# Adding the experts' rows straight into the output tensor, with the seldom steps' branch moved into the last sure step

## The chip, the core and the metric

The kernel runs on one core of a Trainium2 chip. Its engines work side by side, each through its own list of instructions in order: PE (TensorE, matmuls; its weight loads are a row of their own, PEld), DVE (VectorE), ACT (ScalarE), POOL (GpSimd) and SP (SyncE, which here only issues transfers). Engines wait for each other through semaphores. The metric is the time of one execution on the device in microseconds (us); the median of three runs stands for the kernel before.

## The reference: what is computed

One decoder layer on `x` of 8 batch rows x 256 tokens x 256 features, and a context of the same shape, all float32:

```python
x = x + linear_attention(layernorm(x))                   # 16 heads, phi(q), phi(k) = elu + 1
x = x + cross(layernorm(x), ctx)                         # l2norm(q) * sum(l2norm(k) * v) @ Wfc + ctx
residual = x
xn = layernorm(x) * gamma + beta
probs = softmax(xn @ Wg.T)                               # 8 experts
top1, top2 = the two likeliest experts; gates g1, g2 = their shares of p1 + p2
out = x + layernorm(x) + sum over e of gate[e] * (gelu(xn @ W1[e] + b1[e]) @ W2[e] + b2[e])
```

Each token goes to exactly two of eight experts, so the last part is 4,096 pairs of a token and an expert, each a product with a 256 x 1024 and a 1024 x 256 matrix. Only the last sum, `residual + out`, is touched by the change: how the experts' rows reach the output.

## The kernel before

**Rows, then steps.** The first part goes through the batch rows (256 tokens each) in a software pipeline: a loop over rounds `i` from 1 to 7 (L1011) calls the stages of rows `i`, `i-1`, `i-2` and `i-3` one after another. PE, DVE, ACT and SP keep the order of the source; POOL's order is chosen by the compiler, save where `in_turn` (L289) ties an instruction to the one before it. The second part is a list of steps (`steps`, L930): in each, 128 pairs of one expert are pushed through both matrices. Steps are interleaved into the last rows' stages by `meanwhile`, and then run alone.

**Slots.** `rank` (L690) counts on PE how many earlier tokens chose each expert, and `place` (L703) turns that into a slot number: 2,048 slots for each of 8 experts, 128 to a tile. Four indirect transfers from POOL per batch row (`slots<-pay,posi`, L726) write token number and gate into the slots. Slots that nobody fills keep what `empty_slots` (L239) wrote at the start: token numbers 2048 to 2175, which are 128 rows of padding behind the real ones, and gate 0.

**A step** s: `fetch_slots` (L844) loads 128 slots, `fetch_weights` (L852) loads the expert's first matrix (1 MB) and second bias; `gather` (L865) collects the 128 token rows from `rows_d`, a DRAM copy of the normalised rows; `turn` (L872) transposes them on PE; eight `first_chunk` (L887) matmul pairs with a gelu on ACT each; eight `second_chunk` (L905) matmuls, run one step later, chunk by chunk between the next step's first chunks; `add_out` (L914) adds the bias on DVE, scales by the gate on ACT, and an indirect transfer from POOL adds the 128 rows into `acc` (L921). `acc` is a DRAM buffer of 2,048 + 128 rows that `base` (L598) has filled with x + layernorm(x) before. An add must wait until the add before it has landed, since both may hold the same token.

**The end.** There can be 32 to 39 steps, as the tokens fall. The first 36 are always run (`SURE`, L927; a step too many works on empty slots). After them every engine reads the number of steps (L1137) and jumps over the three seldom steps if it is 36 or less (L1141), as with this input. Then SP copies `acc` into the output, 2 MB from DRAM to DRAM (L1150), and the program closes (recorded under L1182): SP waits for all transfers, all engines drain and meet.

The functions that the change touches, and what calls them:

Of the kernel before, what the change touches and what calls it, by code (L numbers as in the profile page):

```python
# [29 lines left out]
def decoder_kernel(  # L30
# [59 lines left out]
    rows_d = dram.tile([NTOK + P, D], F32, name="rows_d")  # L90
    acc = dram.tile([NTOK + P, D], F32, name="acc")
# [97 lines left out]
    zero = const("zero", [P, D])  # L189
# [6 lines left out]
    def iota_f(t, shape, pattern):  # L196
        ti = const(t.name + "_i", shape, I32)
        nc.gpsimd.iota(ti, pattern=pattern, base=0, channel_multiplier=0)
        nc.vector.tensor_copy(t, ti)
# [38 lines left out]

    def empty_slots():  # L239

        nc.gpsimd.memset(pads, 0)
        nc.gpsimd.iota(pads[:, :, 0], pattern=[[1, P]], base=NTOK, channel_multiplier=0)
        nc.gpsimd.memset(zero, 0.0)
        nc.sync.dma_start(slots[0 : NTILE - 1, :], pads[:, :, :].rearrange("p r c -> p (r c)"))
        nc.sync.dma_start(
            slots[NTILE - 1 : NTILE, :], pads[0:1, :, :].rearrange("p r c -> p (r c)")
        )
        nc.sync.dma_start(rows_d[NTOK:, :], zero)
        nc.sync.dma_start(acc[NTOK:, :], zero)
# [348 lines left out]
    def base(st):  # L598
        b = st["b"]
        x3 = st["x2"]  # L600
        for t in range(T):
            nc.scalar.activation(
                x3[:, t, :], x3[:, t, :], AF.Identity,
                bias=st["sb"][:, 1, t : t + 1], scale=st["sb"][:, 0, t : t + 1],
            )
        nc.sync.dma_start(tokens(acc, b), x3)
# [6 lines left out]
    puts = []  # L613
# [88 lines left out]

    def place(st):  # L703

        new = named(st)
        at = st["b"] * T
        hot = st["hot"]
        slot = new("slot", [P, T, E])
        nc.vector.tensor_tensor(
            slot,  # L710
            st["prank"].rearrange("p (t e) -> p t e", e=E),
            slot0[:, None, :].to_broadcast([P, T, E]),
            ALU.add,
        )
        nc.vector.tensor_tensor(
            hot, hot, slot[:, :, None, :].to_broadcast([P, T, 2, E]), ALU.mult
        )
        pos = new("pos", [P, T, 2])
        nc.vector.tensor_reduce(pos, hot, axis=AX.X, op=ALU.add)
        posi = new("posi", [P, T, 2], I32)  # L720
        nc.vector.tensor_copy(posi, pos)
        earlier = list(behind)
        behind.clear()
        for t in range(T):
            for c in range(2):
                put = nc.gpsimd.indirect_dma_start(  # L726
                    out=slot_rows,
                    out_offset=bass.IndirectOffsetOnAxis(ap=posi[:, t, c : c + 1], axis=0),
                    in_=pay[:, at + t, c, :], in_offset=None,
                )  # L730
                tc.declare_no_dep(
                    put.ins, group="slots", reason="every token and choice has a slot of its own"
                )
                tc.add_to_no_dep_group("slots", put.ins)
                for name in earlier:
                    tc.add_manual_dep(put.ins, name, ORDERED, reason="in the order of the source")
                puts.append(put.ins.name)
                behind.append(put.ins.name)
# [112 lines left out]

    def fetch_weights(s):  # L852
        e_sp = said(s, 0, ET.SP)
        w1s[s] = mpool.tile([P, KD, F], F32, tag="w1", name=f"w1_{s}", bufs=3)
        nc.sync.dma_start(
            w1s[s], w1_rows[bass.ds(e_sp * D, D), :].rearrange("(k p) f -> p k f", p=P)
        )
        b2s[s] = mpool.tile([P, D], F32, tag="b2", name=f"b2_{s}", bufs=3)
        nc.sync.dma_start(b2s[s], b2_flat[bass.ds(e_sp * D, D)].partition_broadcast(P))

    def reach(s):

        return RA * S if s < NA else NTOK + P
# [8 lines left out]
    def turn(s):  # L872
        p = ps(f"pt_{s}")
        xg = xgs.pop(s)
        for k in range(KD):
            nc.tensor.transpose(p[:, k * P : (k + 1) * P], xg[:, k * P : (k + 1) * P], ident)  # L876
        ready[s] = mpool.tile([P, KD, P], F32, tag="xgT", name=f"xgT{s}")
        for k in range(KD):
            nc.vector.tensor_scalar(  # L879
                ready[s][:, k, :], p[:, k * P : (k + 1) * P],  # L880
                gamma_c[:, k : k + 1], beta_c[:, k : k + 1], op0=ALU.mult, op1=ALU.add,
            )
# [3 lines left out]

    def first_chunk(s, c):  # L887
        if c == CHUNKS[0]:
            hT = mpool.tile([P, FC, P], F32, tag="hT", name=f"hT{s}")
            p = [wide(f"ph_{s}_{i}").rearrange("p (c n) -> p c n", n=P) for i in range(2)]  # L890
            hidden[s] = hT, p, said(s, 0, ET.Activation)
# [3 lines left out]
        for k in range(KD):  # L895
# [5 lines left out]
            hT[:, c, :], p, AF.Gelu_apprx_tanh,  # L901
# [3 lines left out]
    def second_chunk(s, c):  # L905
        if c == CHUNKS[0]:
            summed[s] = ps(f"py_{s}"), said(s, 0, ET.PE)
        p, e_pe = summed[s]
        nc.tensor.matmul(  # L909
            p[:, 0:D], hidden[s][0][:, c, :], w2_flat[:, bass.ds((e_pe * FC + c) * D, D)],  # L910
            start=(c == CHUNKS[0]), stop=(c == CHUNKS[-1]),
        )

    def add_out(s):  # L914
# [6 lines left out]
        in_turn(nc.gpsimd.indirect_dma_start(  # L921
            out=acc[0 : reach(s), :],
            out_offset=bass.IndirectOffsetOnAxis(ap=ids.pop(s)[:, 0:1], axis=0),
            in_=yg[:, :], in_offset=None, compute_op=ALU.add,
        ))
# [4 lines left out]
    def steps(first, last):  # L930
# [3 lines left out]
        for s in range(first, last + 1):  # L934
# [7 lines left out]
            for j, c in enumerate(CHUNKS):  # L942
                took = 0.0
# [14 lines left out]
            yield took  # L958

# [51 lines left out]
    for i in range(1, B):  # L1011
# [7 lines left out]
        run(add_context, i - 2)  # L1019
        run(gates, i - 3)  # L1020
# [9 lines left out]
        run(attend, i - 1)  # L1030
        run(place, i - 3)
        if i > 1:
            run(first_norm, i + 1)
# [14 lines left out]
        if i == 2:  # L1048
            gate_row()
        run(cross_out, i - 2)  # L1050
# [5 lines left out]
        run(key_powers, i)  # L1056
        run(last_norms, i - 2)
        run(attention_out, i - 1)
# [4 lines left out]
        run(turn_last, i - 2)  # L1063
        run(second_norm, i - 1)
# [26 lines left out]
    run(place, p - 1)  # L1091
    run(attended, q)
# [23 lines left out]
    run(place, p)  # L1116
    run(add_context, q, True)
# [15 lines left out]
    run(place, q)  # L1133
    step_end()
    plans["b"] = plan_steps("b", B - 1, NSTEP - NA, other_tiles)
    meanwhile(1e6)
    n_steps = nc.values_load(  # L1137
        total[0:1, 0:1], min_val=0, max_val=NSTEP,
        skip_runtime_bounds_check_because=CLAMPED,
    )  # L1140
    with tc.If(n_steps > SURE):  # L1141
        for s in range(SURE, NSTEP):
            fetch_slots(s)
            fetch_weights(s)
        for s in range(SURE, NSTEP):
            gather(s)
        turn(SURE)
        for _ in steps(SURE, NSTEP):
            pass
    nc.sync.dma_start(out.rearrange("b s d -> (b s) d"), acc[0:NTOK, :])  # L1150

# [34 lines left out]
```

## Time and profile before

| what | value |
|---|---|
| median of 3 runs | 463.07 us (461.97 to 465.4) |
| the profiled execution, its own time | 466.37 us |
| its span in the profile | 464.2 us |
| mean granted TensorE clock | 0.985 |
| PE busy in the span | 435.6 us |
| rounds 3, 4 and 5 over the batch rows | 20.7, 20.8 and 20.7 us |
| a step, from 240 us on | 7.25 us |
| last matmul ends | 447.8 us |
| last add into `acc` starts | 450.30 us |
| copy to the output issued | 454.16 us |

The profile is of one execution, told from the start of its span; the execution's own time is 2.2 us longer, since some of it lies outside the span. PE's matmuls overlap their weight loads, and the ends of matmuls are modelled. [...] A q behind an engine (PEq, POOLq) means its sequencer, which reads instructions ahead of the engine and takes jumps, register loads and drains itself. "Records" are the instructions that the profiler wrote down.

### The profile page before, as it was taken

The page shows a single profiled execution, that of the slowest core. Times are in us where ns is not written, and L with a number is a line of the kernel's source. Part 1 is how long each engine was busy: PE and PEld are TensorE (multiplying, and loading weights), DVE is VectorE, ACT ScalarE, POOL GpSimd, SP SyncE. Part 2 cuts the span into 40 slices and gives each one's busy share as a digit, 9 for nine tenths or more (in the row PEclk, how much of TensorE's full clock was granted, in tenths as well). Part 3 has the DMA queues.
Part 4 walks back from the last instruction along what each step waited for, and adds up shares of the span by engine and source line. Part 5 has one row for each costly group of instructions (what it writes and reads, how often), then busy time and mean ns, then how long its engine had stood idle before and what let it go on. Part 6 is the DMA issues. An engine that isn't in the chain of part 4 may idle for free.

```text
span 464.2 us, 8501 instructions
## 1 busy us (share of the span) xinstructions
PE 435.6 (94%) x2671; PEld 369.7 (80%) x2671; DVE 184.0 (40%) x692; ACT 214.0 (46%) x551; POOL 187.2 (40%) x201
## 2 busy tenths in 40 slices
PE   8889999999999999988999999999999999999950
PEld 5557687776857689877999999899999999999950
DVE  2556778787888767454111110111101111011100
ACT  3526455464636454443444444444444444444420
POOL 6305264536445653635433324333342433333220
PEclk9999999999999999999999999999999999999995
DMA  8604266755604163786677676676757767668225
GB/s 231 202 2 136 69 204 57 217 100 173 137 1 145 28 171 123 182 237 127 157 230 205 177 235 179 200 201 187 233 161 222 194 192 220 185 209 220 41 26 191
DMA packets 48368, 74.36 MB, mean 160 GB/s; under 512 B 9774, under 2 KB 37811, under 8 KB 48291
## 3 DMA queue, kind: packets, MB, share of 16 engines
q1 hardware_dynamic: 39298, 63.10, 46.2%
q0 software_dynamic: 8208, 9.91, 11.3%
q10 hardware_dynamic: 816, 0.79, 0.5%
q8 instruction: 24, 0.39, 0.4%
q14 instruction: 22, 0.17, 0.1%
HBM read 64.44 MB, written 11.44 MB: 163 GB/s over the span
## 4 chain that ended last, share of the span: by engine, by line
PE 86%; DVE 5%; ACT 2%; issue 1%; DMA 1%; POOL 1%; another core or an unknown queue 1%; POOLq 0%; ACTq 0%; DVEq 0%
PE ph L896 28%; PE py L909 26%; PE pxkv L344 6%; PE pkv L344 4%; PE pq L407 3%; PE pq L344 3%; PE po L344 3%; PE pfc L344 3%; PE pt L876 2%; PE pt L338 1%; PE pstate L472 1%; PE pstate L457 1%; DVE qT L421 1%; PE plog L344 1%; PE ptc L338 1%
## 5 line engine op out<-in xcount | busy, mean ns | idle before, releaser
L896 PEld LDWEIGHTS ph<-xgT,w 128*128 128x128 f32 x1152 | 167.2, 191 | 20.2 <-ACT hT L900 4.2
L896 PE MATMUL ph<-xgT,w 128*128 128x128 f32 x1152 | 175.6, 276 | 3.4 <-ACT hT L900 2.4
L909 PE MATMUL py<-w_s,hT 128*128 x576 | 170.7, 380 | 0.0
L900 ACT ACTIVATE hT<-ph,vcols 128x128 f32<-128x128 f32 x288 | 103.0, 367 | 120.5 <-PE ph L896 106.5
L921 POOL DMA_INDIRECT acc<-yg,ids x36 | 57.1, 1586 | 151.3 <-ACT hT L900 113.7
L879 DVE TENSOR_SCALAR xgT<-pt,vcols 128x128 f32<-128x128 f32 x72 | 26.2, 406 | 158.7 <-PE pt L876 150.7
L909 PEld LDWEIGHTS py<-w_s,hT 128*128 128x128 f32 x576 | 88.1, 192 | 0.4
L867 POOL DMA_INDIRECT xg<-rows_d,ids x36 | 36.1, 1002 | 11.7 <-issue 6.2
L726 POOL DMA_INDIRECT slots<-pay,posi x32 | 32.1, 1003 | 10.4 <-issue 7.7
L918 DVE TENSOR_TENSOR y<-py,b 128x256 f32<-128x256 f32 x36 | 15.3, 425 | 44.8 <-ACT hT L900 32.9
L344 PE MATMUL pxkv<-xwkv_s,cT 128*128 128x512 f32 x64 | 31.8, 624 | 0.7 <-ACT cT L378 0.7
L344 PE MATMUL pkv<-wkv_s,hT 128*128 128x512 f32 x64 | 29.9, 593 | 0.0
L920 ACT ACTIVATE yg<-y,ids 128x256 f32<-128x256 f32 x36 | 18.3, 508 | 23.2 <-DVE y L918 21.5
L344 PEld LDWEIGHTS pxkv<-xwkv_s,cT 128*128 128x128 f32 x64 | 12.0, 198 | 10.1 <-issue 8.7
L306 POOL TENSOR_TENSOR rs_b<-ve_b,mhalf 128x2 f32<-128x2 f32 x8 | 8.2, 1021 | 24.4 <-DVE ve_b L319 24.4
L344 PEld LDWEIGHTS po<-wo_s,turnedoT 128*128 128x128 f32 x64 | 12.0, 190 | 7.1 <-ACT turnedoT L508 3.0
L344 PEld LDWEIGHTS pkv<-wkv_s,hT 128*128 128x128 f32 x64 | 11.1, 190 | 8.2 <-issue 8.1
L344 PE MATMUL po<-wo_s,turnedoT 128*128 128x256 f32 x64 | 15.3, 381 | 2.1 <-ACT turnedoT L508 2.1
L407 PE MATMUL pq<-hT,wq_s 128*128 128x256 f32 x64 | 15.2, 381 | 0.6 <-ACT hT L383 0.6
L306 POOL TENSOR_TENSOR rs_a<-ve_a,mhalf 128x2 f32<-128x2 f32 x8 | 5.7, 707 | 24.2 <-DVE ve_a L319 24.2
L344 PE MATMUL pq<-xwq_s,turnedx2T 128*128 128x256 f32 x64 | 15.2, 380 | 0.0
L344 PE MATMUL pfc<-xwfc_s,turnedq2T 128*128 128x256 f32 x64 | 15.2, 380 | 0.0
(193 smaller groups left out, 510.5 us busy)
## 6 DMA issues: line engine op xcount, KB each, us to landing
w<-in_L_ffn_W_dram SPq DMA_DIRECT2D x36, 1024.0 KB
w_s<-in_L_ffn_W_dram SPq DMA_DIRECT2D x8, 1024.0 KB
b<-in_L_ffn_b_dram SPq DMA_DIRECT2D x36, 128.0 KB
x<-in_x_dram SPq DMA_DIRECT2D x8, 256.0 KB
rows_d<-h SPq DMA_DIRECT2D x8, 256.0 KB
acc<-x SPq DMA_DIRECT2D x8, 256.0 KB
c<-in_ctx_dram SPq DMA_DIRECT2D x7, 256.0 KB
ids<-slots SPq DMA_DIRECT2D x36, 1.0 KB
```

Source lines behind the costliest of these rows:

```text
L306: in_turn(nc.gpsimd.tensor_tensor(dst, src, mhalf[:, 0:n], ALU.pow))
L344: nc.tensor.matmul(p[:, 0:width], srcT[:, k, t * P : (t + 1) * P], w[:, k, 0:width], start=(k == 0), stop=(k == KD - 1),)
L407: nc.tensor.matmul(p[:, m, :], wq_s[:, k, m * P : (m + 1) * P], st["hT"][:, k, :], start=(k == 0), stop=(k == KD - 1),)
L726: put = nc.gpsimd.indirect_dma_start(out=slot_rows, out_offset=bass.IndirectOffsetOnAxis(ap=posi[:, t, c : c + 1], axis=0), in_=pay[:, at ...
L867: in_turn(nc.gpsimd.indirect_dma_start(out=xgs[s][:, :], out_offset=None, in_=rows_d[0 : reach(s), :], in_offset=bass.IndirectOffsetOnAxis ...
L879: nc.vector.tensor_scalar(ready[s][:, k, :], p[:, k * P : (k + 1) * P], gamma_c[:, k : k + 1], beta_c[:, k : k + 1], op0=ALU.mult, op1=ALU ...
L896: nc.tensor.matmul(p, w1s[s][:, k, c * P : (c + 1) * P], ready[s][:, k, :], start=(k == 0), stop=(k == KD - 1),)
L900: nc.scalar.activation(hT[:, c, :], p, AF.Gelu_apprx_tanh, bias=vcols[:, bass.ds(e_act * FC + c, 1)],)
L909: nc.tensor.matmul(p[:, 0:D], hidden[s][0][:, c, :], w2_flat[:, bass.ds((e_pe * FC + c) * D, D)], start=(c == CHUNKS[0]), stop=(c == CHUNK ...
L918: nc.vector.tensor_tensor(y, p[:, 0:D], b2s.pop(s), ALU.add)
L920: nc.scalar.activation(yg, y, AF.Copy, scale=ids[s][:, 1:2].bitcast(F32))
L921: in_turn(nc.gpsimd.indirect_dma_start(out=acc[0 : reach(s), :], out_offset=bass.IndirectOffsetOnAxis(ap=ids.pop(s)[:, 0:1], axis=0), in_= ...
```

## The change

Four things change together.

1. `acc` goes. `base` writes x + layernorm(x) into the output tensor itself, the indirect transfers add into it, and the copy at the end is left out. `rows_d` loses its 128 rows of padding too.
2. Since there is no padding row left, an empty slot must name a real token that has nothing to do with the expert's tile, with gate 0: two slots of one transfer must not name the same token. The empty slots of all tiles get tokens 0 to 127 at the start. An expert's first tile can hold some of these for real, so once row 0's choices are known, its 128 slots are filled with tokens of row 0 that did not choose the expert: `without`, `spread` and `fill_spare` find them with DVE comparisons and 16 small bf16 matmuls in round 3, and a transfer writes them. Row 0's puts come after that, in round 4, in two pairs (`put` is split off from `place`).
3. The read of the number of steps and the jump over the seldom steps move from the end into step 35, the last sure one, ahead of its third chunk. The seldom steps run there one after another, with shared buffers (`own`).
4. The program ends with a memset on POOL that waits for the landing of the last add.

```diff
-    rows_d = dram.tile([NTOK + P, D], F32, name="rows_d")
-    acc = dram.tile([NTOK + P, D], F32, name="acc")
+    rows_d = dram.tile([NTOK, D], F32, name="rows_d")
+    out_rows = out.rearrange("b s d -> (b s) d")
...
+        nc.vector.tensor_copy(tok, pay[:, 0:T, 0, 0])
+        iota_f(back, [P, P], [[-1, P]], P - 1)
+        for t in range(T):
+            nc.vector.tensor_tensor(
+                tok_e[:, t],
+                eye8[:, :, None].to_broadcast([P, E, E]),
+                eye8[:, None, :].to_broadcast([P, E, E]),
+                ALU.is_equal,
+            )
+            nc.vector.tensor_scalar_mul(tok_e[:, t], tok_e[:, t], tok[:, t : t + 1])
...
-        nc.gpsimd.iota(pads[:, :, 0], pattern=[[1, P]], base=NTOK, channel_multiplier=0)
-        nc.gpsimd.memset(zero, 0.0)
+        nc.gpsimd.memset(spare, 0)
+        nc.gpsimd.iota(pads[:, :, 0], pattern=[[1, P]], base=0, channel_multiplier=0)
...
-        nc.sync.dma_start(rows_d[NTOK:, :], zero)
-        nc.sync.dma_start(acc[NTOK:, :], zero)
...
-        nc.sync.dma_start(tokens(acc, b), x3)
+        bases.append(nc.sync.dma_start(tokens(out_rows, b), x3).ins.name)
...
+    def without(st):
+        free = small.tile([P, T, E], BF16, tag="free", name="free")
+        nc.vector.tensor_tensor(
+            free,
+            tok[:, :, None].to_broadcast([P, T, E]),
+            st["prank"].rearrange("p (t e) -> p t e", e=E),
+            ALU.subtract,
+        )
+        nc.vector.scalar_tensor_tensor(
+            free, st["both"], -2.0 * S, free, op0=ALU.mult, op1=ALU.add
+        )
+        st["at"] = mpool.tile([P, T, E, P], BF16, tag="w1", name="at", bufs=3)
+        st["free"] = free
+
+    def spread(st, t):
+        nc.vector.tensor_tensor(
+            st["at"][:, t],
+            back[:, None, :].to_broadcast([P, E, P]),
+            st["free"][:, t, :, None].to_broadcast([P, E, P]),
+            ALU.is_equal,
+        )
+
+    def fill_spare(st):
+        p = ps("pspare")
+        for t in range(T):
+            for e in range(E):
+                nc.tensor.matmul(
+                    p[0:E, 0:P], tok_e[:, t, e, :], st["at"][:, t, e, :],
+                    start=(t == 0 and e == 0), stop=(t == T - 1 and e == E - 1),
+                )
+        nc.vector.tensor_copy(spare[:, :, 0], p[0:E, 0:P])
+        nc.sync.dma_start(
+            slots[0 : NTILE - 1, :].rearrange("(e q) c -> e q c", e=E)[:, 0, :],
+            spare.rearrange("e r c -> e (r c)"),
+        )
...
+    def put(st, *ts):
+        at, posi = st["b"] * T, st["posi"]
...
-        in_turn(nc.gpsimd.indirect_dma_start(
-            out=acc[0 : reach(s), :],
+        add = nc.gpsimd.indirect_dma_start(
+            out=out_rows[0 : reach(s), :],
...
+        in_turn(add)
+        sums.append(add.ins.name)
...
             for j, c in enumerate(CHUNKS):
+                if s == SURE - 1 and j == 2:
+                    seldom()
...
+    def seldom():
+        n_steps = nc.values_load(
+            total[0:1, 0:1], min_val=0, max_val=NSTEP,
+            skip_runtime_bounds_check_because=CLAMPED,
+        )
+        with tc.If(n_steps > SURE):
+            for s in range(SURE, NSTEP):
+                fetch_slots(s)
+            for s in range(SURE, NSTEP):
+                gather(s)
+            for s in range(SURE, NSTEP):
+                fetch_weights(s)
+                turn(s)
+                for c in CHUNKS:
+                    first_chunk(s, c)
+                for c in CHUNKS:
+                    second_chunk(s, c)
+                add_out(s)
...
         run(add_context, i - 2)
+        if i == 4:
+            put(rows[0], 0)
...
         run(attend, i - 1)
+        if i == 3:
+            without(rows[0])
         run(place, i - 3)
+        if i > 3:
+            run(put, i - 3)
...
+        if i == 3:
+            spread(rows[0], 0)
         run(cross_out, i - 2)
...
         run(key_powers, i)
+        if i == 3:
+            spread(rows[0], 1)
         run(last_norms, i - 2)
+        if i == 4:
+            put(rows[0], 1)
...
         run(turn_last, i - 2)
+        if i == 3:
+            fill_spare(rows[0])
...
-    n_steps = nc.values_load(
...
-        for _ in steps(SURE, NSTEP):
-            pass
-    nc.sync.dma_start(out.rearrange("b s d -> (b s) d"), acc[0:NTOK, :])
+    nc_last = nc.gpsimd.memset(mhalf, 0.0)
+    tc.add_manual_dep(nc_last.ins, sums[-1], WRITTEN, reason="the last rows are added")
```

## The prediction

> **What bounds the kernel now.** I read the busy times and their slices first, then the last pieces of the chain of waits, then the waits of SP's queue, and last the instructions of the lines that the change moves.
>
> ```profile
> PE 435.6 (94%) x2671; PEld 369.7 (80%) x2671; DVE 184.0 (40%) x692; ACT 214.0 (46%) x551; POOL 187.2 (40%) x201
> ...
> 57.40:78.10 20.70, 20.45 (x108) 15.40 (x108) 16.28 (x65) 11.37 (x29) 11.21 (x13) 1.00 0.59 140
> 119.60:141.70 22.10, 21.23 (x109) 15.33 (x109) 18.88 (x83) 11.30 (x29) 11.27 (x14) 1.00 0.21 46
> 240.00:440.00 200.00, 199.92 (x1377) 184.61 (x1376) 31.60 (x83) 93.05 (x249) 68.92 (x53) 1.00 0.67 192
> ```
>
> The three window rows read: length, then PE, weight loads, DVE, ACT and POOL busy. PE is full in the rounds over the batch rows (20.45 of 20.70) and in the steps (199.92 of 200), so work added to PE costs its own time, and DVE work costs what PE then waits for it.
>
> ```profile
> 445.70 3.86 DMA acc<-yg,ids
> ...
> 450.60 1.25 POOL acc L921
> ```
> ```profile
> SPq L1150 <- DMA acc<-yg,ids: 19.5, 1, 19.5
> ...
> SPq L1182 <- DMA out_dram<-acc: 7.5, 1, 7.5
> ```
>
> After the last matmul (447.8) nothing computes. The add of step 34 lands 3.86 us after its start, at 449.56; the last add starts at 450.30 and lands at 454.16, when SP's wait of 19.5 ends; the copy's issue is 0.61, its landing another 7.5, and the rest to 464.2 is 1.5. From last landing to end: **10.06 us**.
>
> **What goes: the copy (L1150).** All of it lies on the path. What is late next is POOL's own closing:
>
> ```profile
> L1182 POOLq DRAIN  x3: 46/103/5953, 452.7 to 463.9; - x3
> ...
> L1141 POOLq INC_SWDGE_SEM  x1: 1593/1593/1593, 451.1 to 451.1; - x1
> ```
>
> One of three drains takes 5.95 us. It must be the first (at 452.7): a later one would overrun the span. It ends at 458.67, hidden under the copy, and the closing exchange after the copy's landing needs 1.1 from POOL. The change queues it behind a memset that waits for the last landing. Bounds: 0 (it falls away, or runs beside the landing) to 5.95 (it starts after the memset). The nearest row is its own, and it stands behind the memset in POOL's order, so I take 5.95. From last landing to end: 0.4 until the memset has run (0.10 by L141's row, the start as after the add's landing at 449.56, rounded down), 5.95, 1.1, in all 7.45. **Gain 10.06 - 7.45 = 2.6**; with no drain 10.06 - 1.6 = 8.5.
>
> [...]
>
> **What comes: the branch inside step 35.** Before, the jump over the seldom steps came when PE had nothing left to issue:
>
> ```profile
> L1141 PEldq COMPARE_BRANCH  x1: 3634/3634/3634, 444.8 to 444.8; - x1
> L1141 SPq COMPARE_BRANCH  x1: 45/45/45, 431.4 to 431.4; - x1
> ...
> L1141 ACTq COMPARE_BRANCH  x1: 45/45/45, 448.7 to 448.7; - x1
> ...
> q8 instruction: 24, 0.39, 0.4%
> ```
>
> PE's took 3.63 us, the others' 0.05 to 0.07. Queue q8 moved 24 packets of 16 KB, one per some 240 of PE's records (5,779 in all), so it is PE's instruction fetch; a 3.63 us jump is one that waits for such a fetch. The arm skipped is three steps of 110 records and some waits, about 340 records or 1.4 fetches.
>
> At the new place PE's sequencer stands ahead of PE: in the trace the address step of a step's second L909 chunk comes 1.45 us before the weight load that uses it, steady over steps 4 to 34. With that chunk's 0.43 it has 1.88 us in hand. It spends 0.57 until the branch is read (444.24 to 444.81 in the end now), the branch, and 0.3 on the arm's semaphores; the first of these also waits until PE's own matmuls are done. Dear jump: 0.57 + 3.63 + 0.3 - 1.88 = 2.6 of idle PE. Cheap jump: only the emptied pipeline, about 0.17 for the last matmul's end, 0.3 for the semaphores, 0.1 to the next weight load: 0.6. Both rows are near (PE's own; the four others' same instruction). What decides is whether the landing place has been fetched. By record counts the jump now starts about 86 records earlier in its fetched stretch (some 120 records of steps 35 and 36 then come behind it, 34 new ones of the spare rows ahead). [...] I take the cheap one, **0.6**, and keep 2.6 as the upper end, 0.5 as the lower.
>
> [...]
>
> The join's POOL part (TENSOR_LOAD 0.51, INC_SWDGE_SEM 1.59) falls between the adds of steps 33 (438.68 to 440.23) and 34 (445.70): 5.5 us of idle cover it; without it the last two adds come later one for one. ACT's and DVE's 0.4 to 0.9 lie in ACT's 0.51 per chunk and DVE's 6.6 idle.
>
> **What comes: the spare rows, before step 0.**
> - Tables (two copies, four 128x64 operations): DVE 1.2, by six rows of about 0.2 (L219, L228). They stand ahead of k at L446, which waits 0.46 for ACT anyway and must be done by 21.73 for PE's pstate: k ends 21.9 instead of 21.2. **0.25**.
> - Sixteen bf16 matmuls of 128 columns on PE in round 3. No row shows one; fp32 transposes of 128 columns follow each other by 0.11 (four in 0.44), and bf16's weight load is half fp32's (0.096 against 0.19): 0.055 to 0.11 each, 0.9 to 1.8. The load's row is the nearer: **1.1**, all on PE.
> - DVE in round 3: two small operations 0.35, two of 1,024 elements (0.42 at 256 and 0.69 at 512 elements give 1.23 each), a copy 0.2: 3.0 us. The round at 119.6 has the plan's 4.0 us of DVE in one piece and is 1.4 longer than its neighbours. Here it is in four pieces, before PE has taken 1.1 more itself and DVE idles 0.93, 0.53, 1.04 and 0.51: 0 to 1.0, **0.25**.
>
> ```profile
> 76.10 1.07 POOL L306 TENSOR_TENSOR rs_b<-ve_b,mhalf 128x2 f32<-128x2 f32 x1 [3.00 <-DVE ve_b L319]
> ...
> 83.92 0.71 POOL L306 TENSOR_TENSOR rs_a<-ve_a,mhalf 128x2 f32<-128x2 f32 x1 [3.39 <-DVE ve_a L319]
> ```
>
> - Row 0's four puts (1.0 each, 0.3 between) move a round later, two into POOL's 3.39 idle before rs_a, two into the 3.00 before rs_b: 2.6 each, hidden. The first waits for the spare slots' transfer: SP issues it near 78 (the copy's end), between the base rows (75.2) and the next load, whose second half waits until 80.6 now. If it lands by 81, POOL is in time; rs_a, and with it DVE's off and ACT's h, stand behind it. Cost 0; if the cover is gone, up to 2 us.
> - POOL's new iota replaces a memset (0.3) in an idle of 3.96; two 128 KB writes go, at 14.8 and 15.6, with SP idle. 0.
>
> **Sum.** -2.6 + 0.6 + 0.25 + 1.1 + 0.25 = **-0.4 us**: span 463.8 for 464.2, and 466.0 for the profiled execution's 466.37. On the median of 463.07 (the profiled one is 0.7% above it): **462.7**. Bounds with the long drain: 461.9 to 466.
>
> **Rivals.**
> - B1, the drain runs beside the last landing, from the last add's issue: 450.7 + 5.95 + 1.1 = 457.7, plus 2.2 of costs: span 459.9, time 458.8. For it: the drain now begins at 452.7, before the landing at 454.16. Against: POOL's own work had ended at 451.8.
> - B2, the drain is short: 454.16 + 0.5 + 1.3 = 455.9, plus 2.2: span 458.1, **457.0**. For it: two POOL drains take 0.05 and 0.10. Against: they follow one that had just cleared up.
> - C, slower: the jump in step 35 waits for its fetch again. PE stands 2.6, 2.0 more than taken; with the long drain the span is 465.8 and the time **464.7**, +0.3%. It decides as soon as the jump's stall exceeds 1.0. For it: PE's only row. Against: the shift by 86 records.
> - D, it does not do what it says about order: the output is no tile of the pool, so adds might no longer wait for each other. The last would start at 449.1 rather than 450.3: 1.2 less, 461.5. The wait row of 3.0 before L921 would be gone. 1 in 10, within the cases below.
> - E, POOL late in round 4 and the stall handed on through rs_a in each round after: over 5 us, 468.
>
> **How the numbers follow.** Long drain with a cheap jump 0.38 (462.7, its range 461 to 464.5), with a dear one 0.15 (464.7); B1 0.17 (458.8, with a dear jump 460.8); B2 with a cheap jump 0.17 (457.0), with a dear one 0.06 (459.0); E 0.07. About 1% (4.6 us) is what a measurement of this kernel tells from no change. Faster by over 1%, under 458.4: B2 cheap, a quarter of B1 and a third of B2 dear: 0.24. Slower by over 1%: E, 0.07. The rest 0.69. The range, 456.8 to 465.3, leaves out E and the lower half of B2.
>
> **What would show it.** The copy's row is gone, and the wait of 7.5 at L1182. A POOL drain of about 6 us starts after the last landing (B1: earlier; B2: below 0.2). PE's COMPARE_BRANCH is below 0.1 (C: about 3.6), with an idle stretch of 0.6 (C: 2.6) between two L896 groups near 440. Round 3 is 1.1 to 2.1 longer, the others as they were. rs_a still waits for DVE in round 4, not for the slots. I am wrong above all if the drain's 5.95 us does not come back.

## The result and the profile after

The changed kernel took 461.62 us (median of 22 runs, 459.41 to 464.12) where the kernel before took 463.17 (22 runs, 461.23 to 466.71): ratio 0.9956, 95% interval 0.9937 to 0.9976, some 2.0 us less. The forecast was 462.7, range 456.8 to 465.3. The profiled execution has a span of 461.4 (464.2 before).

The page of the changed kernel: sixteen operations of PE, eleven of DVE and two of POOL are what is added, and PE's instruction fetch is 24 packets as before.

```profile
PE 437.3 (95%) x2687; PEld 372.2 (81%) x2687; DVE 187.8 (41%) x703; ACT 214.0 (46%) x551; POOL 187.6 (41%) x203
...
q8 instruction: 24, 0.39, 0.3%
```

**The tail.** The end of the chain of waits (start, length, what), then the rows of the closing lines (what is written from what, minimum, median and maximum in ns, first and last start), then SP's waits (total, times, longest), all of the changed kernel:

```profile
448.47 0.52 ACT yg L997
448.99 1.56 issue
450.55 3.75 DMA out_dram<-yg,ids
...
454.34 0.37 issue
454.70 0.11 POOLq L1289
```
```profile
L1257 POOL MEMSET mhalf<- x1: 101/101/101, 454.7 to 454.7; 128x4 f32 x1
...
L1289 POOLq DRAIN  x3: 46/109/5802, 454.7 to 461.1; - x3
```
```profile
SPq L1289 <- DMA out_dram<-yg,ids: 21.0, 2, 16.5
```

The copy and its wait of 7.5 are gone. The last add lands at 454.30, the long drain starts at 454.70 and takes 5.80, and the span ends at 461.36: 7.05 us from the last landing to the end (10.06 before). The last row says something that the diff does not: SP's closing waits for the same landing by itself, so by this row GpSimd's memset guards nothing that was open. No run leaves it out.

**The branch.** Rows of the branch's line and the stretch of PE around it (start, busy time, in brackets PE's idle time before and what ended it):

```profile
L1048 PEldq COMPARE_BRANCH  x1: 1292/1292/1292, 437.1 to 437.1; - x1
...
L1048 POOLq INC_SWDGE_SEM  x1: 1545/1545/1545, 439.1 to 439.1; - x1
```
```profile
438.12 0.60 PE L986 MATMUL py<-w_s,hT 128*128 x2
439.01 0.68 PE L973 MATMUL ph<-xgT,w 128*128 128x128 f32 x4 [0.30 <-PEq L1048]
```

PE's jump took 1.29 us, neither 0.05 nor 3.63, and PE stood for a moment only. The exact loss: from step 34's first weight load for the second matmul to the last one of all there are 10.25 us here and 9.72 before, so 0.53.

**The spare rows.** The sixteen matmuls in PE's order, then the windows of rounds 3 and 4 as this execution has them (length, then PE, weight loads, DVE, ACT and POOL busy, PE's clock, DMA share, GB/s):

```profile
77.26 0.60 PE L351 MATMUL pt<-ident,h 128*128 128x128 f32 x4
77.79 1.06 PE L744 MATMUL pspare<-at,tok_e 128*8 128x128 bf16 x16
78.78 1.98 PE L357 MATMUL pxkv<-xwkv_s,cT 128*128 128x512 f32 x4
```
```profile
59.40:81.30 21.90, 21.65 (x125) 16.29 (x125) 18.80 (x70) 11.26 (x29) 7.13 (x9) 1.00 0.42 134
81.30:102.00 20.70, 20.45 (x108) 15.41 (x108) 16.29 (x65) 11.37 (x29) 15.43 (x17) 1.00 0.73 152
...
240.00:440.00 200.00, 199.70 (x1376) 184.43 (x1375) 31.55 (x83) 93.00 (x249) 69.44 (x54) 1.00 0.67 192
```

Round 3 is 1.2 us longer than its 20.70 of before, and PE was busy in all of that (21.65 against 20.45). Round 4 has its 20.70 although POOL carries four puts more. GpSimd is still waiting for VectorE, not for the spare slots:

```profile
85.50 0.98 POOL L780 DMA_INDIRECT slots<-pay,posi  x1 [0.30 <-issue]
87.34 0.72 POOL L319 TENSOR_TENSOR rs_a<-ve_a,mhalf 128x2 f32<-128x2 f32 x1 [0.86 <-DVE ve_a L332]
```

So far each term is where the prediction has it. What does not fit is in between. Against the profile of before, steps 0 and 1 of the changed profile are 3.4 us late (start of step 0's second chunks: 181.13 against 177.76), steps 2 and 3 are 2.8 late, and from step 4 on they are 0.04 early. PE was busy 38.69 us of the 40 from 200 to 240, and 37.69 before. Either the steps absorb what the front costs, which would make the spare rows free, or the two executions differ by something that is in neither kernel. That, and the size of each term, is what the experiments are for.

Theory A: the change is worth the sum of tail, branch and sixteen matmuls; the rest of the two profiles' difference is accident. Theory B: something between 190 and 225 us waits for a fixed time and swallows the front's cost.

### The profile page after: what moved, and what is told of

Read it like the earlier page. It is cut to its first block, busy times and chain, and to the rows that moved or that the text cites. A ratio compares the mean times of both kernels' runs of the same rounds, so it can differ in the third digit from the quotient of the medians.

```text
span 461.4 us, 8548 instructions
## 1 busy us (share of the span) xinstructions
PE 437.3 (95%) x2687; PEld 372.2 (81%) x2687; DVE 187.8 (41%) x703; ACT 214.0 (46%) x551; POOL 187.6 (41%) x203
## 5 line engine op out<-in xcount | busy, mean ns | idle before, releaser
L998 POOL DMA_INDIRECT out_dram<-yg,ids x36 | 57.2, 1588 | 147.7 <-ACT hT L977 106.3
L357 PE MATMUL pxkv<-xwkv_s,cT 128*128 128x512 f32 x64 | 30.4, 600 | 0.8 <-DMA xwkv_s<-in_L_xattn_Wv_dram 0.8
L357 PE MATMUL po<-wo_s,turnedoT 128*128 128x256 f32 x64 | 16.7, 408 | 2.1 <-ACT turnedoT L521 2.1
L420 PE MATMUL pq<-hT,wq_s 128*128 128x256 f32 x64 | 16.6, 406 | 0.6 <-ACT hT L396 0.6
L319 POOL TENSOR_TENSOR rs<-ve,mhalf 128x4 f32<-128x4 f32 x8 | 8.3, 1034 | 18.8 <-DVE ve L593 18.8
L377 ACT ACTIVATE h<-x,off,rs_a 128x256 f32<-128x256 f32 x16 | 8.7, 592 | 14.8 <-DVE off L374 14.8
```

What stands on the lines that cost most here:

```text
L319: in_turn(nc.gpsimd.tensor_tensor(dst, src, mhalf[:, 0:n], ALU.pow))
L357: nc.tensor.matmul(p[:, 0:width], srcT[:, k, t * P : (t + 1) * P], w[:, k, 0:width], start=(k == 0), stop=(k == KD - 1),)
L420: nc.tensor.matmul(p[:, m, :], wq_s[:, k, m * P : (m + 1) * P], st["hT"][:, k, :], start=(k == 0), stop=(k == KD - 1),)
L998: add = nc.gpsimd.indirect_dma_start(out=out_rows[0 : reach(s), :], out_offset=bass.IndirectOffsetOnAxis(ap=ids.pop(s)[:, 0:1], axis=0), i ...
```

## The experiments

All ratios are to the kernel before, run on the same chip in the same stretch; its median there was 468.64 us in the first four runs, 467.09 in the next four, 463.18 in the two with 56 and 84 gathers, 465.96 in the last two.

### 1. Both kernels again

`after_again` is the changed kernel and `before_again` the kernel before, without edits.

> The changed kernel once more, beside the kernel before on the same chip, for a second profile of it. Theory A (three terms make the result: tail -2.96, the jump's stall +0.44, the sixteen matmuls of round 3 +1.18, the rest nothing): ratio to before about 0.997, and again a POOL DRAIN of 5.8 us that starts after the last landing, PE's COMPARE_BRANCH near 1.3 us and step 0's second chunks 1.2 us later than before, measured from the start of round 2. Theory B (the steps give the front's cost back, because something from 190 to 225 us waits for a fixed time): PE stands less between 190 and 225 us than it does before, in this profile too, and the ratio is nearer to 0.994.

> The kernel before once more, for a second profile of it. If the 3.4 us of idle PE between 195 and 217 us that its first profile has and the changed kernel's has not (ScalarE standing 2.52 us for something that the profile doesn't name, among others) belongs to the kernel, it is here again; if it was an accident of that execution, PE is busy there for all but some 1.5 us. PE's COMPARE_BRANCH is again near 3.6 us, POOL's first closing DRAIN near 5.95.

The changed kernel: 467.04, ratio 0.997 (0.9941 to 0.9999). The drain is again 5.80 and behind the landing. From 200 to 240 us, changed kernel again and kernel before again:

```profile
200.00:240.00 40.00, 36.73 (x241) 33.25 (x242) 13.09 (x60) 16.96 (x45) 16.20 (x14) 0.96 0.69 168
```
```profile
200.00:240.00 40.00, 36.05 (x235) 31.97 (x234) 14.12 (x62) 16.52 (x44) 16.17 (x14) 0.96 0.72 163
```

Both stand here, by the same stall: ScalarE waits for something that the profile doesn't name and PE with it. ScalarE and PE of the changed kernel, then ScalarE of the kernel before:

```profile
216.76 0.37 ACT L977 ACTIVATE hT<-ph,vcols 128x128 f32<-128x128 f32 x1 [3.23 <-remote]
...
217.18 0.49 PE L973 MATMUL ph<-xgT,w 128*128 128x128 f32 x2 [2.45 <-issue]
```
```profile
219.39 0.37 ACT L900 ACTIVATE hT<-ph,vcols 128x128 f32<-128x128 f32 x1 [3.24 <-remote]
```

It belongs to both kernels, and the first profile of the changed one was an execution without it. Theory B loses its ground: from the first of the four transposes near 200 us to the first of step 5's there were 24.5 us in the first profile of before and 21.6 in that of the changed kernel, but 26.5 in the new profile of either. (`before_again` took 471.56 in its one run; its drain is again 5.95 and PE's jump 3.57.)

### 2. Without the spare rows

```diff
-                if s == SURE - 1 and j == 2:
+                if s == SURE - 1 and j == 5:
...
-        if i == 4:
-            put(rows[0], 0)
...
-        if i == 3:
-            without(rows[0])
         run(place, i - 3)
-        if i > 3:
-            run(put, i - 3)
+        run(put, i - 3)
...
-        if i == 3:
-            fill_spare(rows[0])
```

(the tables, both calls of `spread` and the second `put` of row 0 go in the same way)

> Leaves out the filling of the spare slots: the tables, the free rows, the sixteen matmuls and the slots' transfer, with the first row's puts back in their old round, so that empty slots of the experts' first tiles name other tokens than they should; the branch stands three chunks later in its step, so that PE meets it at the same place of its instruction stream as in the changed kernel. Theory A: round 3 is 1.18 us shorter on PE, every step starts 1.2 us earlier than in the changed kernel, and the time is 1.2 us less, ratio to before about 0.993 (0.994 to 0.991). Rival (the front's cost is absorbed between 190 and 225 us): the steps from 4 on start when they do in the changed kernel, and the time is the same as that of the changed kernel. POOL's puts of the first row are again between 57 and 78 us, and round 4's POOL work is back at 11.1 us.

465.41, ratio 0.9928 (0.9897 to 0.9959): 2.0 us below the changed kernel on the same chip by the two ratios, with intervals that overlap. Round 3 of this kernel:

```profile
59.40:80.10 20.70, 20.45 (x108) 15.40 (x108) 16.26 (x65) 11.37 (x29) 11.16 (x13) 1.00 0.56 140
```

It is 1.2 shorter than the changed kernel's and equal to the 20.70 of before, and the steps keep the lead: over the same transposes near 200 us to step 5's this profile has 26.5 us, as the others of this chip. The front's cost goes through to the end. Theory A holds for round 3: 1.18 us, all of it PE's sixteen matmuls; DVE's work in that round and the moved puts cost nothing that shows.

The tables do cost something, but not in the profile read so far, where PE's clock was halved just ahead of that place, from 18.61 to 22.02 us (last section). The transposes `ptc` near 20 us and the matmuls `pstate` behind them, in the first profile of before and in `dve_end`, a variant of the changed kernel (section 4) whose clock was whole there; last, DVE's k in `dve_end`:

```profile
21.13 0.60 PE L338 MATMUL ptc<-ident,c 128*128 128x128 f32 x4
21.57 1.09 PE L457 MATMUL pstate<-v,k 128*128 128x136 f32 x8
```
```profile
19.60 0.60 PE L351 MATMUL ptc<-ident,c 128*128 128x128 f32 x4
20.15 1.19 PE L470 MATMUL pstate<-v,k 128*128 128x136 f32 x8
```
```profile
19.41 0.69 DVE L459 SCALAR_TENSOR_TENSOR k<-k,tmpexk 128x512 f32<-128x512 f32 x1
```

With the tables ahead of it, k ends at 20.10, and PE's first weight load for `pstate` starts at 20.15 after 0.18 of idle. From these `ptc` to the `ptc` at the start of round 3 there are 36.39 to 36.41 us in the five profiles with tables and a whole clock there, and 36.17 or 36.18 in the two without tables: **0.21 us**. The spare rows as a whole cost 1.4.

### 3. The tail alone

The kernel before, its copy left out; the base rows are written to the output as well as to `acc`, where the experts' sums stay:

```diff
         nc.sync.dma_start(tokens(acc, b), x3)
+        nc.sync.dma_start(out[b].rearrange("(t p) d -> p t d", p=P), x3)
...
-    nc.sync.dma_start(out.rearrange("b s d -> (b s) d"), acc[0:NTOK, :])
+    nc_last = nc.gpsimd.memset(mhalf, 0.0)
+    tc.add_manual_dep(nc_last.ins, sums[SURE - 1], WRITTEN, reason="the last rows are added")
```

> The kernel before with the last copy left out, so that the output holds the rows of the base alone (each base row is written to the output too) and the experts' sums stay in the scratch buffer; a memset on GpSimd waits for the last add's landing, as in the changed kernel. This is the tail's part of the change alone. Theory A: from the last add's start to the end 10.85 us instead of 13.9, a POOL DRAIN of 5.8 to 5.95 behind the memset, 3.0 us less, ratio to before 0.9935 (0.991 to 0.997). Rival (the long drain was a thing of the copy or of the join right ahead of it): no POOL drain above 0.2 us, 8.5 us less, ratio 0.982.

463.43, ratio 0.994 (0.9912 to 0.9969): 2.8 us less. From the last add's start to the end 10.67 us (13.93 in the first profile of before, 13.75 in the second), and the drain stands behind the memset, as long as ever:

```profile
L1186 POOLq DRAIN  x3: 46/109/5802, 452.5 to 458.9; - x3
```

So the tail is worth 2.8 to 3.3, and the drain is no thing of the copy.

### 4. The last wait on VectorE, and the branch at the end

```diff
-    nc_last = nc.gpsimd.memset(mhalf, 0.0)
+    nc_last = nc.vector.memset(upto_a, 0.0)
```

> The wait for the last add's landing is given to a small memset on VectorE instead of GpSimd; all else as in the changed kernel. Theory A (POOL's closing drain is a fixed piece of work of 5.8 us that needs no landing and only stood behind the memset): the drain starts right behind the last add's issue, near 452.1 in the changed kernel's time, ends near 457.9, and the span ends 0.95 later: 2.5 us less than the changed kernel, ratio to before about 0.990. Rival (the drain itself waits for the landing of what POOL has issued): it starts at 452.1 but ends 5.8 after the landing, no gain against the changed kernel.

465.36, ratio 0.9933 (0.9898 to 0.9969). From the last add's start to the end 9.44 instead of 10.81 us: 1.4 less, not the 2.5 expected, and not nothing. (PE's mean clock was 0.975 in the profiled execution; only its tail is read.)

```profile
L1289 POOLq DRAIN  x3: 46/109/8498, 458.6 to 467.9; - x3
```

The record starts 0.23 ahead of the last add's own start (458.79), so it holds the add too. It ends 8.27 after the add's start. If the drain's own part is 5.80 as elsewhere, it begins 2.5 after that start, where I had put it at 1.55, the length of the add's row.

`dve_end` has the same (its memset waits for the add of step 35 and for that of the last seldom step), and the branch behind the last step again:

```diff
-                if s == SURE - 1 and j == 2:
-                    seldom()
     meanwhile(1e6)
+    seldom()
```

> VectorE's memset has the last wait, as in the run before, and the branch stands behind the last step again, as in the kernel before; the spare rows stay. Theory A (the branch inside step 35 costs PE 0.44 us of its own; at the end GpSimd's half of the join, some 2 us, lies beside what GpSimd does anyway for 2.4 us between the last add's start and the 5.8 us of the drain): PE has no gap of 0.86 us between two weight loads in step 35, its COMPARE_BRANCH is 3.6 us again where nothing waits for it, the last add's start to the end stays at 9.4 us, and the time is 0.4 us below the run with VectorE's memset alone: ratio to before about 0.992. Rival (the join on GpSimd puts the drain off one for one): the last add's start to the end is 11.5 us, ratio about 0.997.

464.21, ratio 0.9944 (0.9907 to 0.998): by time not to be told from the run before it. In the trace the two theories part: from the last add's start to the end 9.56 us, so GpSimd's half of the join costs 0.1 at most, and PE has its 9.71 from step 34's first second-matmul load to the last instead of 10.25. With the join ahead of it the drain's row holds the drain alone. It starts right behind INC_SWDGE_SEM, 2.4 after the add's start at 450.07 and ahead of the add's landing at 453.75, and is as long as ever (5.84), so it waits for no landing:

```profile
L1289 POOLq DRAIN  x3: 46/252/5842, 452.5 to 459.4; - x3
...
L1046 PEldq COMPARE_BRANCH  x1: 3574/3574/3574, 444.6 to 444.6; - x1
...
L1046 POOLq INC_SWDGE_SEM  x1: 1593/1593/1593, 450.9 to 450.9; - x1
```

### 5. What a jump costs PE

```diff
-                if s == SURE - 1 and j == 2:
+                if s == SURE - 1 and j == 0:
```

> The branch stands two chunks earlier in step 35, ahead of its first chunk; all else as in the changed kernel. In the six profiles so far PE's jump ended 2.5 to 2.7 us after the first packet of PE's instruction queue for the stretch it lands in, or 0.4 after it began where that packet was long past. In the two profiles of the changed kernel that packet came 1.2 us ahead of the jump, so a jump 1.8 us earlier comes before it. Theory A: PE's COMPARE_BRANCH takes 2.5 to 3.6 us, the sequencer's lead at that place (1.0 to 1.4 us) doesn't cover it, and PE stands 2.2 to 3.3 us in step 35 instead of 0.44. Rival (a jump ahead of the last steps is never dear, whatever has been fetched): 0.4 to 1.6 us and PE stands at most 1.0.

466.81 in one run. Two chunks earlier in the same step the jump is dear, and PE stands for it:

```profile
L1048 PEldq COMPARE_BRANCH  x1: 2892/2892/2892, 437.3 to 437.3; - x1
```
```profile
440.66 0.68 PE L973 MATMUL ph<-xgT,w 128*128 128x128 f32 x4 [2.08 <-PEq L1048]
```

Some 2.3 us lost between the two weight loads (2.65 apart, 0.32 at the same place one step earlier) for 0.53 in the changed kernel. Beside the records of PE's instruction queue q8 the lengths fall in line:

| kernel | first packet | jump starts | jump takes | end - packet |
|---|---|---|---|---|
| before | 445.79 | 444.81 | 3.63 | 2.65 |
| before_no_copy | 444.09 | 443.09 | 3.65 | 2.65 |
| dve_end | 445.61 | 444.62 | 3.57 | 2.59 |
| branch_j0 | 437.80 | 437.30 | 2.89 | 2.39 |
| after_again | 438.65 | 439.80 | 1.57 | 2.72 |
| after | 435.94 | 437.11 | 1.29 | 2.45 |
| no_spare_j5 | 442.43 | 445.10 | 0.46 | 3.13 |
| close_dve | 438.20 | 445.19 | 0.36 | 7.36 |

The packet is the last that started before the jump ended. A jump ends 2.4 to 2.7 us after that packet, or about 0.4 after its own start where the packet is long past. And PE loses the same 0.53 or 0.54 in all seven profiles with the branch at the third or sixth chunk of step 35, whether the jump took 0.36 or 1.57: the sequencer's lead, 1.88 us by the trace of before, covers that much, and what is left is, by the rows of the changed kernel, PE's 0.30 of idle until the arm's semaphores are through, and the emptied pipeline around it: the group of py ahead (0.60 long) runs to its end, where it is overlapped by 0.16 elsewhere (next start 0.44 behind its own), and from the group of ph behind to the next there are 0.52 instead of 0.44.

The lengths read as a jump that waits for the fetch which that packet begins, and that may also meet it half way, as with the 1.29 and 1.57 of the changed kernel, 1.17 and 1.15 behind the packet. What they do not bear out is a place fixed by the count of instructions, as the forecast took it: `close_dve` has the changed kernel's stream on PE, and its packet came 7.0 us ahead of the jump instead of 1.2.

### 6. What the drain depends on

`more_pool_dma`: the changed kernel with one more gather per step.

```diff
+            if 5 <= s < 33:
+                again = mpool.tile([P, D], F32, tag="xg2", name=f"again{s}", bufs=1)
+                in_turn(nc.gpsimd.indirect_dma_start(
+                    out=again[:, :], out_offset=None, in_=rows_d[0 : reach(s), :],
+                    in_offset=bass.IndirectOffsetOnAxis(ap=ids[s][:, 0:1], axis=0),
+                ))
```

> The changed kernel with 28 more gathers issued by GpSimd, one in each of steps 5 to 32, into a tile that nothing reads; GpSimd has 4 us free in each step for 1.0 of issue. If the closing drain is work per transfer that GpSimd has issued (5.80 us for 111 of them is 52 ns each), it is now 7.2 to 7.3 us; if it is fixed, it stays at 5.8.

Both wrong: more transfers, shorter drain.

```profile
L1295 POOLq DRAIN  x3: 46/109/3518, 458.7 to 462.8; - x3
```

464.89 in one run, from the last add's start to the end 8.19. Next, narrow gathers (8 bytes a row), two and three (`range(3)`) in each of steps 5 to 32, in all 56 and 84:

```diff
+                for _ in range(2):
+                    again = mpool.tile([P, 2], I32, tag="again", name=f"again{s}", bufs=8)
+                    in_turn(nc.gpsimd.indirect_dma_start(
+                        out=again[:, :], out_offset=None, in_=slot_rows[0 : reach(s), :],
+                        in_offset=bass.IndirectOffsetOnAxis(ap=ids[s][:, 0:1], axis=0),
+                    ))
```

> The changed kernel with 56 more gathers on GpSimd (two in each of steps 5 to 32), of 8 bytes a row instead of 1 KB, into tiles that nothing reads. The 28 gathers of 1 KB a row made the closing drain shorter, 3.52 us instead of 5.80: 81 ns less for each. Theory A (what the drain does falls with the number of transfers issued, whatever their size): 5.80 - 56 x 0.081 = 1.2 us, from the last add's start to the end 6.2 us instead of 10.8, and 4.6 us less than the changed kernel if the gathers hide: ratio to before about 0.987. Rival 1 (it falls with the bytes moved or the width of the rows): 5.8 us, less some 0.05. Rival 2 (it isn't a straight line, but runs round, as a ring would): a value off 1.2 that the next run of this call helps to place.

> As the run before, with 84 such gathers, three in each of steps 5 to 32. Theory A: 71 transfers more bring the drain to nothing, so with 84 it is below 0.3 us and stays there, or, if what it does runs round (rival 2), it jumps up again to many microseconds. Rival 1 (by bytes): 5.8 us. If three gathers in a step don't hide on GpSimd (3.0 of issue and 0.9 between, beside 2.6 of its own, in 7.25), steps are longer by what is over.

With 56 the ratio is 0.9973 (0.9948 to 0.9999) and from the last add's start to the end there are 10.39 us; with 84, 464.38 in one run. The drain's rows of the one and of the other:

```profile
L1296 POOLq DRAIN  x3: 46/109/5682, 452.9 to 459.1; - x3
```
```profile
L1296 POOLq DRAIN  x3: 46/109/4294, 457.4 to 462.3; - x3
```

Theory A (a straight fall) is out. The last two runs add the same narrow gathers to `dve_end`, two in each of steps 5 to 28 (`best_48`) and one in each of steps 5 to 32 (`best_28`):

> VectorE's memset last and the branch at the end, with 48 narrow gathers on GpSimd (two in each of steps 5 to 28). The drain was 5.80 us without, 3.52 with 28 gathers of 1 KB rows (1344 packets more on GpSimd's queue), 5.68 with 56 narrow ones (1792 packets) and 4.29 with 84 (2688). Theory A (it falls by 1.70 ns a packet and starts anew every 2.9 to 3.05 us of it, some 1750 packets): 48 narrow gathers are 1536 packets, 2.6 us less, a drain of 3.2 us, from the last add's start to the end 6.9 us instead of 9.5, ratio to before about 0.988. Rival (it goes by the number of transfers: 81 ns for each up to 54, then anew): 3.9 us less, 1.9 us, ratio 0.985. If neither, the drain is off both values, and what it does stays open.

> As the run before with 28 narrow gathers, one in each of steps 5 to 32. By packets (896 at 1.70 ns): a drain of 4.3 us, ratio to before about 0.991. By transfers (28 at 81 ns): 3.5 us, as with the 28 wide ones, ratio 0.989.

| gathers added | transfers issued by GpSimd | drain, us |
|---|---|---|
| 0 | 111 | 5.80 to 5.95 |
| 28 of 1 KB rows | 139 | 3.52 |
| 28 narrow | 139 | 3.38 |
| 48 narrow | 159 | 4.89 |
| 56 narrow | 167 | 5.68 |
| 84 narrow | 195 | 4.29 |

Size is out: 28 wide and 28 narrow ones give the same within 0.14, in two kernels whose drains without gathers differ by 0.04. By packets, 28 narrow ones should have left 4.3, and 48 left 3.2; by transfers falling 81 ns each, 48 should have left 1.9. None holds but the single value of 3.5 at 28. From 139 to 167 transfers the drain grows by 0.08 us for each, and it falls at least once below and once above that stretch. Six points don't settle what makes it so; that stays open. The join's INC_SWDGE_SEM on GpSimd goes with it: 1.55 to 1.59 us beside drains of 5.80 to 5.95, 1.51, 1.39 and 1.15 beside 5.68, 4.89 and 4.29, and 1.02 and 0.96 beside 3.38 and 3.52. In the kernels with the branch in step 35 it runs over 10 us ahead of the drain, so what sets the length seems to be there, for the most part, before the last two adds.

**`best_28` beats both kernels**: 458.95 us, ratio 0.9857 (0.9822 to 0.9891), against 0.9956 for the change and 0.997 for `after_again`, each beside the kernel before on its own chip. From the last add's start to the end it has 6.08 us, with a GpSimd that is done 1.5 us after the landing:

```profile
451.00 3.76 DMA out_dram<-yg,ids
...
454.87 0.06 DVE upto_a L1263
```
```profile
L1053 POOLq INC_SWDGE_SEM  x1: 1015/1015/1015, 451.8 to 451.8; - x1
...
L1296 POOLq DRAIN  x3: 46/103/3380, 452.9 to 456.8; - x3
```

`best_48` does not: 465.21, ratio 0.9987 (0.996 to 1.0015). Its tail is 7.97, 1.6 shorter than that of `dve_end`, but PE stood in the steps, by ScalarE:

```profile
PE ph L973 <- ACT hT L977: 4.4, 5, 1.7
```

The 56 gathers, two a step as well, show no such row over 0.2 us in their profile. From step 5 to step 34 `best_48` takes 3.8 us more than `best_28` (214.27 against 210.47, first second-matmul loads). Its twelve runs have their median, 465.21, where the profiled one lies (465.05), so it was hardly that execution alone; but why 48 gathers bring these stalls here and 56 in the changed kernel don't, no run shows.

## Why the prediction was right

- **The drain.** It was to come back, whole, behind the last landing, and to take the copy's place: 0.4 + 5.95 + 1.1 = 7.45 from landing to end, measured 7.05 (0.40 + 5.80 + 0.85). Gain 3.0 for 2.6. Rival B2 is out, by every profile taken. B1 is out for this kernel and true of the one that gives the wait to VectorE; but it was priced from the add's issue plus 0.4, and the drain's work starts some 2.5 after the add's start, so what it is worth is 1.4, not the 3.9 of the rival.
- **The branch.** 0.6 for 0.53: right in what is paid (0.30 until the semaphores are through, the rest by the emptied pipeline). Of the step that got there, one part was off: the jump was to cost either about 0.05 or 3.63. It took 1.29 and 1.57, as the fetch was under way (its packet had started 1.17 and 1.15 ahead of the jump), and the sequencer's 1.88 us in hand covered it. The choice of the cheap row for the sum rested on a count of records, the jump 86 earlier. No run shows that the count decides: in the six profiles with this stream and place of the branch, the packet came 1.2 to 7.0 us ahead of the jump. So the cheap jump was in part luck, and the margin was thin: two chunks earlier rival C is there, with 2.3 us lost where C had 2.6.
- **The spare rows.** Sixteen matmuls 1.1, measured 1.18 (66 ns each by their row of 1.06 for sixteen, between the bounds of 55 and 110). Tables 0.25, measured 0.21, by the path that was named: k comes later and PE's pstate waits for it. DVE in round 3 0.25 of 0 to 1.0, measured nothing: DVE has 18.80 of 21.90 there and PE no wait for it. The moved puts 0, as said; rival E is out.
- **D** is out: the add of step 35 starts 0.76 us after that of step 34 has landed (450.55 and 449.79), as before (0.74), so the adds still wait for each other in the output.
- **The sum.** -3.0 + 0.53 + 1.18 + 0.21 = -1.1 us in the span, for a forecast of -0.4: 0.4 more on the tail, 0.25 for DVE's work that was hidden. One term is in neither: the time of an execution outside its span is 1.80 us in the changed kernel (22 executions) where the forecast kept the 2.2 of before; in the runs of the experiments the kernel before has 2.11 to 2.16 on average, and the kernels without the copy 1.78 to 1.91. What makes that difference no run shows. With its 0.35 the sum is -1.4. The measurement has -2.0 (-2.9 to -1.1) in the first comparison and -1.4 (-2.8 to 0) on the second chip. Added up in the same way, `best_28` comes to -6.8 (measured -6.7) and `best_48`, with its 3.8 lost in the steps, to -1.1 (measured -0.6). Single terms, too, come out by time alone as they do in the traces: tail 2.8 (1.4 to 4.1), spare rows 2.0 (about 0 to 4).
- **What would have misled.** The two first profiles differ by 2.8 us, for a sum of 1.1 in the span, with 3.4 lost in front and given back later. Of the 3.4 only the sixteen matmuls' 1.2 is the change; the rest and the giving back belong to the executions. And the tables' 0.21 seemed to be nothing, because the clock was halved where it had to show.

## What to carry to other kernels

When a wait is removed from the end, ask what else ran beside it and whether the new order puts that behind the new last event: here a drain of 5.8 us stood in the shadow of the copy, and a memset of 0.1 us on the same engine moved all of it into the open. Give a closing wait to an engine that has nothing to do behind it (VectorE in GpSimd's place: 1.4 us less from the last add's start to the end). And before a difference between two profiles is explained, take each again: the steadiest place to read a term is the stretch that holds it alone, with PE's clock whole in it, such as the rounds of 20.70 us here.

## What the runs showed of the hardware

- **GpSimd's closing drain** is 3.38 to 5.95 us long in the profiles, goes up and down with the number of transfers that the engine has issued (5.80 at 111, 3.38 at 139, 5.68 at 167, 4.29 at 195), and hardly depends on their size (3.52 with 28 gathers of 1 KB rows, 3.38 with 28 narrow ones). It needs no landing: in `dve_end` it starts at 452.50, ahead of the last add's landing at 453.75, and takes 5.84; in the changed kernel it starts 0.40 after the landing and takes 5.80. In the first profile of the kernel before, GpSimd's other two closing drains take 0.05 and 0.10 us and those of the other engines 7 to 17 ns.
- **PE's clock** is halved for a while in some executions of the same kernel and not in others: in the first profile of the changed kernel the granted clock is 0.50 from 18.61 to 22.02 us and from 32.26 to 35.67, 3.41 us each, and in its second it is 1.00 from 8 to 40 us. Slices of 5 us in the first (PE's clock is the number after POOL's busy time):

```profile
15.00:20.00 5.00, 3.46 (x13) 2.10 (x12) 4.39 (x19) 2.83 (x5) 1.95 (x2) 0.86 0.62 197
20.00:25.00 5.00, 4.37 (x27) 3.83 (x26) 1.04 (x3) 1.94 (x4) 0.00 (x0) 0.80 0.00 0
...
30.00:35.00 5.00, 3.15 (x8) 2.56 (x9) 1.49 (x5) 2.72 (x5) 0.00 (x1) 0.73 0.00 0
```

  The first profile of the kernel before had 1.00 in all three; its second had 0.86 over 15 to 40 us, as much as two such stretches take off. In the changed kernel's first profile the same eight matmuls of po took 3.41 us instead of 1.99, and the front was 3.0 us longer for such stretches alone (1.3 at pq, 1.4 at po, 0.3 at pxkv, by their distance to the next group in both profiles). Much of the spread goes with it: of the 22 executions of the changed kernel, those with a mean clock of 0.989 and above had spans of 457.6 to 459.9 us, those with 0.982 and 0.983 had 461.4 to 462.3. Ahead of the two stretches PE's idle times were at most 0.8 and 2.1 us, and 2.45 us ahead of slow matmuls from 218 us on in the changed kernel's second profile (four of ph in 1.06 us instead of 0.61); what brings such a stretch on no run shows.
- **ScalarE's stall** between 211 and 222 us (releaser not named) is in profiles of both kernels: 2.52 and 3.24 us in the two of the kernel before, 3.23 in the second of the changed kernel, 3.95 in `no_spare_j5`. In the first of the changed kernel ScalarE waits at most 0.73 us there. What it waits for is open.
